# A selective-scan image network: operands of the scan moved by eight bytes, one third of the products on GpSimd, the remainder of B from TensorE

## The chip, the cores and the metric

The kernel runs on one core of a Trainium2 chip. The metric is the device time of one execution in microseconds (us), the median of several runs. TensorE (PE in the profile) multiplies matrices into PSUM, VectorE (DVE), ScalarE (ACT) and GpSimd (POOL) work on tiles in the on-chip memories, and SyncE (SP) issues the transfers here. Each engine takes its own instructions in order and waits on semaphores for those of the others.

## The reference

Four images of 56 x 56 tokens with 96 channels go through four layers. Layers 0 and 1 each run a selective scan over the tokens in four orders (by rows or by columns, forward or reversed); layers 2 and 3 are linear attention and a small network in a reduced float format. The scan is nearly all of the time. For each of the 192 inner channels d and 16 states s it computes, token by token:

```
dt = softplus(dt_raw @ dtw.T + dtb)          # a size per token and channel
a  = -exp(A_log)                             # a number per channel and state
h  = exp(dt * a) * h + dt * B[s] * u         # the recurrence over tokens
y  = sum over s of h * C[s]                  # plus u * D
```

dt_raw, B and C are linear functions of u, by a matrix of their own for each order.

## The kernel before

**Tiling.** The scan of a layer, image and order is cut into 7 chunks of 448 tokens: 2 layers x 4 images x 4 orders x 7 = 224 chunks. A chunk has 8 rounds: two halves e of 96 channels by four quarters q of the states. A round covers 96 x 4 pairs of channel and state, which lie on 128 partitions in three groups g of 448 tokens (32 channels by 4 states a group). There are 1792 rounds and 5376 scans.

**A round.** `begin` has TensorE spread B over the partitions into the PSUM tile b (`spread_b`, L580; there is one such tile) and makes the tile v of three rows with CS + 2 = 450 elements, of which the tokens are 1 to 448 (TOKENS) and the outer two take the carried state. VectorE multiplies dt*u (du) by b into v for groups 0 and 1 (L673). The third group's product is made ahead by GpSimd from B in SBUF (half 1 of the tile cb, L651), except in the rounds named by OWN, where VectorE makes it as well: 3, 4 and 6 of the eight, or 3 and 4 in images 1 to 3 of layer 1. ScalarE makes the decay exp(dt * a) of each group in the PSUM tiles da (`decay`, L643; one tile a group, so that the decay of a round waits for the scan of the round before). VectorE scans the three groups in place in v (L699). ScalarE keeps the last column (L703) and puts it beside the next chunk's tokens (`carried`, L658). GpSimd multiplies all three groups by C into hc (L709), and TensorE sums hc over the states into y two rounds later (`add_up`, L737). In every fourth round ScalarE moves y to Y (`keep_sums`, L744).

**A chunk's preparation** is laid over the rounds of the chunks before it (`prepare`, `prepare_on_scalar`, `prepare_ahead`). TensorE projects u to the rows of B, C and dt_raw (L428, in the one PSUM tile pp); ScalarE copies them to cf (L467, L469). Rows 64 to 127 of cf hold what is needed of B for `spread_b`, which multiplies cf as bfloat16 (its upper halves): a part as it is, and, in the rows where GpSimd has taken the upper half away (`split`, L593, two instructions a chunk), the remainder, so that the sum keeps B's precision. TensorE makes dt's argument from 12 or 6 rows of cf (`step_size`, L480), ScalarE makes dt from it with Exp and Ln (`softplus`, L489 and L490), and GpSimd multiplies it by u (`times_u`, L496), each twice a chunk, once for each half e. dt and dt*u go to DRAM (`park`, L506) and come back spread over 128 partitions (`spread`, L513), C and B likewise (`fetch`, L521, four transfers for each q).

**Order.** Every engine's instructions stand in the order in which the generator `scans` records them; SP's transfers too. At two places of a round it yields to side work: the other layers' work on other images (`load`, `middle`, `fuse`, `attend`), which is cut into pieces with estimated costs on ScalarE and TensorE. `spend` and `room` let a piece in where the costs of the round leave room. `keep_busy` fills TensorE's spare time with matmuls by zeros (L724), in number WARM less the estimated work. Side work left over when the scans end is done alone, in the tail.

Of the kernel before, what the change touches and what calls it, by code (L numbers as in the profile page):

```python
# [11 lines left out]
F32 = mybir.dt.float32  # L12
# [21 lines left out]
TOKENS = slice(1, CS + 1)  # L34
# [4 lines left out]
OWN = (3, 4, 6)  # L39
OWN_TAIL = (3, 4)  # L40
# [7 lines left out]
WARM, PER_P = 7.3, 1.6  # L48
# [116 lines left out]
class Net:  # L165
    def __init__(self, ctx, tc, aps, at, out):
# [14 lines left out]
        self.U = [self.big.tile([C, L], F32, name=f"U{e}") for e in range(NE)]  # L181
# [65 lines left out]
    def setup(self):  # L247
# [95 lines left out]
        with tc.tile_pool(name="stage", bufs=1) as st:  # L343
# [10 lines left out]
            self.some = self.upper(self.tiles["w128"][:, :CS])  # L354
            self.zeros = const.tile([128, C], BF16, name="zeros")
# [103 lines left out]
    def rows(self, ch):  # L459
# [5 lines left out]
        ch.cf = sp.tile([128, CS], F32, name="cf")  # L465
# [5 lines left out]
    def step_sizes(self, ch):  # L471

        nc = self.nc
        ch.cd = self.dram.tile([2 * NS, CS], F32, tag="cd", name="cd", bufs=3)
        nc.sync.dma_start(ch.cd, ch.cf[: 2 * NS])
        ch.pd = [self.step_size(ch, 0, self.pp())]

    def step_size(self, ch, e, ps):
        rows = slice(32, 32 + RANK[ch.l])
        self.nc.tensor.matmul(ps[:C], ch.par.wt[rows, C * e : C * e + C], ch.cf[rows], start=True, stop=True)  # L480
        return ps[:C]

    def softplus(self, ch, e):

        dt = self.sp.tile([C, CS], F32, name="dtc")
        self.nc.scalar.activation(dt, ch.pd[e], AF.Exp, bias=ch.par.dtb[:, e : e + 1])  # L489
        self.nc.scalar.activation(dt, dt, AF.Ln, bias=1.0)  # L490
        ch.dtc.append(dt)

    def times_u(self, ch, e):

        du = self.sp.tile([C, CS], F32, name="duc")
        self.nc.gpsimd.tensor_tensor(  # L496
            du.rearrange("p (a b) -> p a b", b=HS),
            ch.dtc[e].rearrange("p (a b) -> p a b", b=HS),
            self.in_order(self.U[e], ch.orient, ch.c * CS, CS),
            ALU.mult,  # L500
        )
        ch.duc.append(du)

    def park(self, l, t):
        d = self.dram.tile([C, CS], F32, tag="dd", name="dd", bufs=8)
        self.nc.sync.dma_start(d, t)  # L506
        l.append(d)

    def spread(self, l, d, name):

        t = self.sp.tile([128, NG, CS], F32, name=name)
        for s in range(4):
            self.nc.sync.dma_start(t[32 * s : 32 * s + 32], d.rearrange("(g d) t -> d g t", d=32))  # L513
        l.append(t)
# [9 lines left out]
    def prepare(self, ch, follow, r):  # L524

        if r == 0:
            self.spread(ch.du, ch.dud[1], "du")
            self.spread(ch.dt, ch.dtd[1], "dt")
            self.fetch(ch, 3)
        if follow is None:  # L530
            return
        if r == 1:
            self.step_sizes(follow)
            self.split(follow, 0)
        elif r == 2:
            self.split(follow, 1)
        elif r == 3:
            follow.pd.append(self.step_size(follow, 1, self.pp()))
            self.times_u(follow, 0)
            self.park(follow.dtd, follow.dtc[0])  # L540
        elif r == 4:
            self.times_u(follow, 1)
            self.park(follow.dtd, follow.dtc[1])
            self.park(follow.dud, follow.duc[0])
            self.spread(follow.dt, follow.dtd[0], "dt")
        elif r == 5:
            self.park(follow.dud, follow.duc[1])
            self.spread(follow.du, follow.dud[0], "du")
        if r > 4:
            self.fetch(follow, r - 5)  # L550

    def prepare_on_scalar(self, follow, r):

        if follow is None:
            return
# [778 lines left out]
```

## Time and profile before

| what | value |
|---|---|
| median of 3 runs (lowest, highest) | 8497.21 us (8489.68, 8497.39) |
| span of the profiled execution | 8506.0 us |
| first scan starts, last scan ends | 120 us, 8158 us |
| a chunk of 8 rounds, mean | 35.9 us |
| VectorE busy | 7810.2 us |
| GpSimd busy | 7589.0 us |
| TensorE busy, ScalarE busy | 7442.0 us, 5928.4 us |
| time of the main queue's packets, share of the 16 DMA engines' span | 69.2% |

The profiled execution took 8506.0 us, 9 us over the median. The busy time of an engine is the time in which at least one of its instructions ran; on VectorE the end of one instruction and the start of the next overlap a little. A line of a group reads: source line, engine, operation, output <- inputs with partitions x elements, count, then busy time and mean ns of one, then the engine's idle time just before them and what ended it. A line of waits reads: engine and line that waited, for whom, then us in total, how often, the longest. A line of a stretch has its start and end, its length, then busy us and instruction count for TensorE, its weight loads, VectorE, ScalarE and GpSimd, the granted TensorE clock, the share of the DMA engines and GB/s. A line of the timeline has start, length, engine, line and how many instructions were merged.

### The profile page before, as it was taken

The numbers are of one execution on the slowest core, as the hardware profiler recorded it, in microseconds if no ns is written. First come the engines' busy times: TensorE is split into PE (matmuls) and PEld (weight loads), VectorE is DVE, ScalarE is ACT, GpSimd is POOL, SyncE is SP. The second block draws the span as 40 slices with busy tenths as digits, with TensorE's granted clock in tenths as the row PEclk, the third lists the DMA queues.
The fourth block names the chain that finished last, engine by engine and source line by source line (L and its number), as shares of the span: only waits on it lengthen the run. The fifth ranks groups of instructions, "written<-read, shape, count | busy, mean of one in ns | idle before, by whom it ended". The sixth has DMA issues, their size and how long they took to land. (4 is left out here: it accounts for less than half of the span.)

```text
span 8506.0 us, 120303 instructions
## 1 busy us (share of the span) xinstructions
PE 7442.0 (87%) x33459; PEld 2707.3 (32%) x33459; DVE 7810.2 (92%) x10142; ACT 5928.4 (70%) x12597; POOL 7589.0 (89%) x4075
## 2 busy tenths in 40 slices
PE   6888888898889888898889988998899888998997
PEld 3222223232333223232233223333333333333345
DVE  5999999999999999999999999999999999999941
ACT  5877667676777657776677755667766777667746
POOL 4989999999999999999999999999999999999930
PEclk8888889898999889998899988999899898998986
DMA  5777677677777777776777777666776777767731
GB/s 142 167 186 186 164 186 182 153 173 168 189 172 179 163 182 175 178 171 161 184 180 176 166 174 171 165 164 165 185 177 160 165 173 185 178 156 166 175 83 45
DMA packets 951337, 1417.87 MB, mean 167 GB/s; under 512 B 176578, under 2 KB 943812, under 8 KB 949796
## 3 DMA queue, kind: packets, MB, share of 16 engines
q1 hardware_dynamic: 949888, 1408.37, 69.2%
q8 instruction: 263, 4.31, 0.2%
q14 instruction: 414, 3.39, 0.1%
q10 hardware_dynamic: 772, 1.80, 0.1%
HBM read 1141.42 MB, written 268.14 MB: 166 GB/s over the span
## 5 line engine op out<-in xcount | busy, mean ns | idle before, releaser
L699 DVE TENSOR_TENSOR_SCAN v<-da,v 128x449 f32<-128x449 f32 (+1 forms) x5376 | 5507.6, 1072 | 62.2 <-ACT v L658 36.2
L709 POOL TENSOR_TENSOR hc<-v,cb 128x1344 f32<-128x1344 f32 x1792 | 5166.6, 2884 | 366.5 <-DVE v L699 230.8
L643 ACT ACTIVATE da<-dt,na 128x448 f32<-128x448 f32 x5376 | 3392.7, 633 | 1409.7 <-DVE v L699 1372.7
L673 DVE TENSOR_TENSOR v<-du,b 128x448 f32<-128x448 f32 x4172 | 2331.4, 605 | 164.7 <-PE b L580 68.4
L737 PE MATMUL y<-hc,four 128*32 128x448 f32 x14336 | 1942.7, 617 | 3.7 <-POOL hc L709 3.6
L651 POOL TENSOR_TENSOR v<-du,cb 128x448 f32<-128x448 f32 x1204 | 1373.4, 1141 | 102.0 <-DMA cb<-cd 45.6
L724 PE MATMUL y<-w,zeros 128*96 128x448 bf16 x5117 | 1443.3, 399 | 0.0
L580 PE MATMUL b<-cf,sel 128*128 128x448 bf16 x1792 | 685.2, 382 | 861.9 <-DVE v L673 856.3
L724 PEld LDWEIGHTS <-zeros 128*96 128x96 bf16 x5117 | 631.2, 134 | 1300.0 <-issue 1142.7
L428 PE MATMUL pp<-U,wd 96*128 96x448 f32 x896 | 671.2, 836 | 13.7 <-DMA U<-u 13.7
L737 PEld LDWEIGHTS y<-hc,four 128*32 128x32 f32 x14336 | 297.0, 114 | 1206.0 <-issue 816.8
L733 PE MATMUL y<-Y,ident 96*96 96x448 f32 x672 | 540.2, 893 | 52.2 <-ACT Y L744 33.0
L496 POOL TENSOR_TENSOR duc<-dtc,U 96x448 f32<-96x448 f32 x448 | 559.2, 1248 | 5.1 <-ACT dtc L490 5.1
L881 PE MATMUL ps<-win,dg 64*64 64x220 f32 (+9 forms) x1962 | 507.9, 453 | 0.0
L480 PE MATMUL pp<-cf,wd 12*96 12x448 f32 (+1 forms) x896 | 484.3, 622 | 0.4 <-ACT cf L467 0.4
L703 ACT COPY carry<-v 128x3 f32<-128x3 f32 x1536 | 298.7, 194 | 262.4 <-DVE v L699 260.0
L489 ACT ACTIVATE dtc<-pp,wd 96x448 f32<-96x448 f32 x448 | 279.0, 623 | 273.9 <-PE pp L480 272.7
L593 POOL TENSOR_TENSOR cf<-cf 64x448 f32<-64x448 f32 x448 | 417.1, 931 | 35.3 <-ACT cf L467 0.3
L744 ACT COPY Y<-y 96x448 f32<-96x448 f32 x448 | 339.5, 758 | 39.2 <-PE y L737 37.4
L881 PEld LDWEIGHTS ps<-win,dg 64*64 64x64 f32 (+2 forms) x1962 | 229.7, 158 | 326.2 <-issue 267.4
L580 PEld LDWEIGHTS <-sel 128*128 128x128 bf16 x1792 | 186.7, 104 | 348.9 <-issue 284.5
L733 PEld LDWEIGHTS y<-Y,ident 96*96 96x96 f32 x672 | 116.5, 184 | 550.1 <-ACT da L643 244.2
(411 smaller groups left out, 5954.0 us busy)
## 6 DMA issues: line engine op xcount, KB each, us to landing
cb<-cd SPq DMA_DIRECT2D x3584, 112.0 KB, 4.3
dt<-dd SPq DMA_DIRECT2D x1792, 168.0 KB, 4.3
du<-dd SPq DMA_DIRECT2D x1792, 168.0 KB, 4.2
dd<-dtc SPq DMA_DIRECT2D x448, 168.0 KB, 2.0
dd<-duc SPq DMA_DIRECT2D x448, 168.0 KB, 2.1
U<-u SPq DMA_DIRECT2D x112, 168.0 KB, 4.7
z<-w SPq DMA_DIRECT2D x56, 224.0 KB, 3.2
u<-w SPq DMA_DIRECT2D x56, 224.0 KB, 3.5
```

The source lines that it names most:

```text
L428: self.nc.tensor.matmul(ch.ps.rearrange("p (a b) -> p a b", b=HS), ch.par.wx[:, e], self.in_order(self.U[e], ch.orient, ch.c * CS, CS), st ...
L496: self.nc.gpsimd.tensor_tensor(du.rearrange("p (a b) -> p a b", b=HS), ch.dtc[e].rearrange("p (a b) -> p a b", b=HS), self.in_order(self.U ...
L580: self.nc.tensor.matmul(ps, self.sel[:, q], self.upper(ch.cf), start=True, stop=True)
L643: nc.scalar.activation(da[g][:, TOKENS], ch.dt[e][:, g], AF.Exp, scale=ch.par.na[:, e, q, g : g + 1])
L651: nc.gpsimd.tensor_tensor(v[:, 2, TOKENS], ch.du[e][:, 2], ch.cb[q][:, 1], ALU.mult)
L673: nc.vector.tensor_tensor(v[:, g, TOKENS], ch.du[e][:, g], b, ALU.mult)
L699: nc.vector.tensor_tensor_scan(v[:, g, way], da[g][:, way], v[:, g, way], 0.0, ALU.mult, ALU.add)
L709: nc.gpsimd.tensor_tensor(hc, v[:, :, TOKENS], ch.cb[q][:, 0].unsqueeze(1).to_broadcast([128, NG, CS]), ALU.mult)
L724: self.nc.tensor.matmul(self.y[:C], self.zeros, self.some, start=False, stop=False)
L733: nc.tensor.matmul(o, w, self.in_order(a, ch.orient, ch.c * CS, CS), start=True, stop=False)
L737: nc.tensor.matmul(self.y[32 * n : 32 * n + 32], self.four, hc[:, g], start=n == 3, stop=n == 3 or q == NQ - 1,)
L881: self.nc.tensor.matmul(o[:, a - r0 : e - r0, x0:x1], diag[:, tap], win[:, a + dy - lo : e + dy - lo, x0 + dx : x1 + dx], start=n == 0, st ...
```

## The change

- **Places.** The tile of a round is now h: one row of 1352 elements a partition, in which group g's tokens begin at element 450 g + 2, so eight bytes into the tile; neighbouring groups share the columns between them. dt*u (du) and dt (dtc) get two elements in front by `shifted`; the tiles of C and B (cb), u, hc and the spread dt stay as they are. The scans and da move by one element too (INNER).
- **Third group.** OWN and OWN_TAIL are empty: GpSimd makes the third group's product in all 1792 rounds (L686 of the new file), VectorE two a round (L691).
- **Remainder of B.** `split` is gone. TensorE subtracts the upper half of cf from the projection still standing in PSUM (`less`, a bfloat16 matmul by minus the identity, L586), and ScalarE copies rows 64 to 127, and a round later rows 96 to 127, again to cf (L573). cf has three buffers and is made two rounds earlier.
- **dt*u in one.** The two halves of dt lie in one tile; Exp is made for each half, Ln and the product with u once for both (L491, L504), and each is parked in one transfer.
- **Schedule.** `prepare` is told the round's distance o to the chunk's first round, in place of separate steps for this chunk, the next and the one after. WARM is 6.8 in place of 7.3, and the costs that `spend` is told for the rounds differ. The scratch space for transfers in the compiler's call is made smaller.

```diff
 CR = CW // HS
 NCW = L // CW
 CS = 448
-TOKENS = slice(1, CS + 1)
+ROW = CS + 2
+WIDE = NG * ROW + 2
+INNER = slice(2, CS + 2)
 NCS = L // CS
 RANK = (12, 6)
 NW, LATE_NW = 13, 20
 NWIN = 3
-OWN = (3, 4, 6)
-OWN_TAIL = (3, 4)
+OWN = ()
+OWN_TAIL = ()
 SPARE = (0.9, 2.4)
...
-WARM, PER_P = 7.3, 1.6
+WARM, PER_P = 6.8, 1.6
...
+            self.minus = const.tile([128, 64], BF16, name="minus")
+            nc.vector.tensor_scalar(self.minus[64:], self.ident[64:, 64:], -1.0, None, ALU.mult)
...
-        ch.cf = sp.tile([128, CS], F32, name="cf")
+        ch.cf = sp.tile([128, CS], F32, name="cf", bufs=3)
...
-    def step_sizes(self, ch):
-        nc = self.nc
-        ch.cd = self.dram.tile([2 * NS, CS], F32, tag="cd", name="cd", bufs=3)
-        nc.sync.dma_start(ch.cd, ch.cf[: 2 * NS])
-        ch.pd = [self.step_size(ch, 0, self.pp())]
-    def step_size(self, ch, e, ps):
+    def step_size(self, ch, e):
         rows = slice(32, 32 + RANK[ch.l])
-        self.nc.tensor.matmul(ps[:C], ch.par.wt[rows, C * e : C * e + C], ch.cf[rows], start=True, stop=True)
-        return ps[:C]
+        ch.pd = self.pp()[:C]
+        self.nc.tensor.matmul(ch.pd, ch.par.wt[rows, C * e : C * e + C], ch.cf[rows], start=True, stop=True)
     def softplus(self, ch, e):
-        dt = self.sp.tile([C, CS], F32, name="dtc")
-        self.nc.scalar.activation(dt, ch.pd[e], AF.Exp, bias=ch.par.dtb[:, e : e + 1])
-        self.nc.scalar.activation(dt, dt, AF.Ln, bias=1.0)
-        ch.dtc.append(dt)
-    def times_u(self, ch, e):
-        du = self.sp.tile([C, CS], F32, name="duc")
-        self.nc.gpsimd.tensor_tensor(
-            du.rearrange("p (a b) -> p a b", b=HS),
-            ch.dtc[e].rearrange("p (a b) -> p a b", b=HS),
-            self.in_order(self.U[e], ch.orient, ch.c * CS, CS),
-            ALU.mult,
-        )
-        ch.duc.append(du)
-    def park(self, l, t):
-        d = self.dram.tile([C, CS], F32, tag="dd", name="dd", bufs=8)
-        self.nc.sync.dma_start(d, t)
-        l.append(d)
-    def spread(self, l, d, name):
-        t = self.sp.tile([128, NG, CS], F32, name=name)
+        scalar = self.nc.scalar
+        if e == 0:
+            ch.dtc = self.shifted(C, NE, "dtc", 1)
+        scalar.activation(ch.dtc[:, e], ch.pd, AF.Exp, bias=ch.par.dtb[:, e : e + 1])
+        if e == NE - 1:
+            scalar.activation(ch.dtc, ch.dtc, AF.Ln, bias=1.0)
+    def shifted(self, rows, n, name, bufs=2):
+        t = self.sp.tile([rows, 2 + n * CS], F32, name=name, bufs=bufs)
+        return t[:, 2:].rearrange("p (n t) -> p n t", t=CS)
+    def times_u(self, ch):
+        ch.duc = self.sp.tile([C, NE, CS], F32, name="duc", bufs=1)
+        u = self.both.rearrange("p e (h w) -> p e w h" if ch.orient else "p e (h w) -> p e h w", w=HS)
+        lo = ch.c * CS // HS
+        in_rows = lambda t: t.rearrange("p e (a b) -> p e a b", b=HS)
+        self.nc.gpsimd.tensor_tensor(in_rows(ch.duc), in_rows(ch.dtc), u[:, :, lo : lo + CS // HS], ALU.mult)
+    def park(self, t):
+        d = self.dram.tile([NE, C, CS], F32, tag="dd", name="dd", bufs=6)
+        self.nc.sync.dma_start(d.rearrange("e p t -> p e t"), t)
+        return d
+    def spread(self, t, d):
         for s in range(4):
             self.nc.sync.dma_start(t[32 * s : 32 * s + 32], d.rearrange("(g d) t -> d g t", d=32))
-        l.append(t)
+    def spread_dt(self, ch, e):
+        ch.dt.append(self.sp.tile([128, NG, CS], F32, name="dt"))
+        self.spread(ch.dt[e], ch.dtd[e])
+    def spread_du(self, ch, e):
+        ch.du.append(self.shifted(128, NG, "du"))
+        self.spread(ch.du[e], ch.dud[e])
+    def groups(self, t, at):
+        return t[:, at : at + NG * ROW].rearrange("p (g t) -> p g t", t=ROW)
...
+    def prepare(self, ch, o):
+        nc = self.nc
+        if o == -14:
+            self.parameters(ch)
+        elif o == -12:
+            self.inputs(ch)
+        elif o == -9:
+            ch.cd = self.dram.tile([2 * NS, CS], F32, tag="cd", name="cd", bufs=3)
+            nc.sync.dma_start(ch.cd, ch.cf[: 2 * NS])
+            self.less(ch, 64)
+        elif o == -8:
+            self.less(ch, 96)
+        elif o in (-7, -6):
+            self.step_size(ch, o + 7)
+        elif o == -5:
+            self.times_u(ch)
+            ch.dtd = self.park(ch.dtc)
+        elif o == -4:
+            ch.dud = self.park(ch.duc)
+            self.spread_dt(ch, 0)
+        elif o == -3:
+            self.spread_du(ch, 0)
+        elif o == 0:
+            self.spread_du(ch, 1)
+            self.spread_dt(ch, 1)
+        if -3 <= o <= 0:
+            self.fetch(ch, o + 3)
+    def prepare_on_scalar(self, ch, o):
+        if o == -10:
+            self.rows(ch)
+        elif o in (-9, -8):
+            part = slice(64 if o == -9 else 96, 128)
+            self.nc.scalar.copy(ch.cf[part], ch.ps[part])
+        elif o in (-7, -6):
+            self.softplus(ch, o + 7)
+    def projected(self, ch, o):
+        return () if o not in (-12, -11) else (o + 12,) if not ch.first else (0, 1) if o == -11 else ()
+    def less(self, ch, at):
+        self.nc.tensor.matmul(
+            ch.ps[at:], self.minus[at:, at - 64 :], self.upper(ch.cf[at:]), start=False, stop=True, skip_group_check=True
+        )
...
-    def split(self, ch, n):
-        x = ch.cf[64 + 32 * n :]
-        self.nc.gpsimd.tensor_tensor(x, x, self.upper(x), ALU.subtract)
...
-        da = [self.psum.tile([128, 512], F32, name=f"da{g}")[:, : CS + 2] for g in range(NG)]
+        da = [self.psum.tile([128, 512], F32, name=f"da{g}")[:, : CS + 4] for g in range(NG)]
...
+                nc.scalar.activation(da[g][:, INNER], ch.dt[e][:, g], AF.Exp, scale=ch.par.na[:, e, q, g : g + 1])
...
+        def column(t, at):
+            return t[:, at : at + 2 * ROW + 1 : ROW]
+        def carried(n):
+            if n < len(rounds) and rounds[n][0].step:
+                ch, e, q = rounds[n]
+                nc.scalar.copy(column(hs[n], ROW if ch.rev else 1), ch.par.carry[:, e, q])
+        def kept(n):
             ch, e, q = rounds[n]
+            if ch.step < NCS - 1:
+                nc.scalar.copy(ch.par.carry[:, e, q], column(hs[n], 2 if ch.rev else CS + 1))
+        def own(n):
+            ch, e, q = rounds[n]
+            return NQ * e + q in (OWN_TAIL if ch.l and ch.i else OWN)
+        hs, bs = {}, {}
+        def tokens(t):
+            return self.groups(t, 2)[:, :, :CS]
         def begin(n):
+            if n < len(rounds):
+                ch, e, q = rounds[n]
+                bs[n] = self.spread_b(ch, q)
+                hs[n] = sp.tile([128, WIDE], F32, name="h", bufs=3)
+                if not own(n):
+                    nc.gpsimd.tensor_tensor(tokens(hs[n])[:, 2], ch.du[e][:, 2], ch.cb[q][:, 1], ALU.mult)
+        def products(n):
             ch, e, q = rounds[n]
+            for g in range(3 if own(n) else 2):
+                nc.vector.tensor_tensor(tokens(hs[n])[:, g], ch.du[e][:, g], bs[n], ALU.mult)
+        def scan(n, g):
             ch, e, q = rounds[n]
+            c = 1 if ch.step else 0
+            way = slice(CS + 1 + c, 1, -1) if ch.rev else slice(2 - c, CS + 2)
+            h = hs[n][:, g * ROW :]
+            nc.vector.tensor_tensor_scan(h[:, way], da[g][:, way], h[:, way], 0.0, ALU.mult, ALU.add)
...
             self.half_round()
-            far = afters.get(ch)
             strided = [1.5 + 1.5 * ch.orient] * (r % NQ == 2)
-            if far and self.projected(far, r) in (0, 1):
-                strided.append(1.5 + 1.5 * far.orient)
-            self.spend((0.7, 0, 1.3, 1.3, 0, 0, 0, 0)[r], 1.3 * (r in (1, 3)) + sum(strided))
+            ahead(n, lambda c, _: strided.append(1.5 + 1.5 * c.orient))
+            self.spend((0.6, 0.7, 1.7, 0, 0, 0, 0.7, 0.6)[r], (0.4, 1.3, 1.3, 0, 0, 0, 0, 0.4)[r] + sum(strided))
             yield "F", n, r
-            self.prepare_on_scalar(nexts.get(ch), r)
...
             hc = sp.tile([128, NG, CS], F32, name="hc", bufs=3)
-            nc.gpsimd.tensor_tensor(hc, v[:, :, TOKENS], ch.cb[q][:, 0].unsqueeze(1).to_broadcast([128, NG, CS]), ALU.mult)
+            nc.gpsimd.tensor_tensor(
+                hc, tokens(hs[n]), ch.cb[q][:, 0].unsqueeze(1).to_broadcast([128, NG, CS]), ALU.mult,
+            )
...
-    nc = _bacc.Bacc("TRN2", target_bir_lowering=False, num_devices=1)
+    nc = _bacc.Bacc("TRN2", target_bir_lowering=False, num_devices=1, dynamic_dma_scratch_size=4096)
```

## The prediction

> **What bounds the kernel now.** I read the engines' busy times first, then the table by stretches, the costliest groups, the waits of VectorE, and a timeline of 5 us for what an instruction costs back to back.
>
> ```profile
> PE 7442.0 (87%) x33459; PEld 2707.3 (32%) x33459; DVE 7810.2 (92%) x10142; ACT 5928.4 (70%) x12597; POOL 7589.0 (89%) x4075
> ```
>
> Two engines are nearly full. The stretches show where they are not:
>
> ```profile
> 0.00:120.00 120.00, 81.07 (x247) 46.54 (x248) 19.45 (x86) 49.35 (x76) 12.55 (x20) 0.82 0.44 123
> ...
> 4000.00:5000.00 1000.00, 871.97 (x3863) 291.64 (x3862) 968.09 (x1239) 708.71 (x1449) 937.81 (x494) 0.91 0.74 175
> ...
> 8158.00:8506.00 348.00, 298.86 (x1293) 184.72 (x1291) 48.78 (x91) 179.75 (x409) 27.93 (x25) 0.75 0.17 45
> ```
>
> The third pair of columns is VectorE: 0.97 of each us between the first scan (120) and the last (8158). The head of 120 us and the tail of 348 us are other work. The body is 8038 us; VectorE is busy there for 7810 - 19 - 49 = 7742, so idle for 296; GpSimd for 7549, idle for 489. The waits of VectorE are small and scattered, and hardly any is on GpSimd:
>
> ```profile
> DVE v L673 <- PE b L580: 68.4, 88, 4.3
> DVE v L699 <- ACT v L658: 36.2, 64, 4.1
> ...
> DVE v L699 <- POOL v L651: 21.2, 28, 1.9
> ```
>
> So VectorE sets the pace, with GpSimd 2.4% behind it. The groups of both:
>
> ```profile
> L699 DVE TENSOR_TENSOR_SCAN v<-da,v 128x449 f32<-128x449 f32 (+1 forms) x5376 | 5507.6, 1072 | 62.2 <-ACT v L658 36.2
> L709 POOL TENSOR_TENSOR hc<-v,cb 128x1344 f32<-128x1344 f32 x1792 | 5166.6, 2884 | 366.5 <-DVE v L699 230.8
> L673 DVE TENSOR_TENSOR v<-du,b 128x448 f32<-128x448 f32 x4172 | 2331.4, 605 | 164.7 <-PE b L580 68.4
> L651 POOL TENSOR_TENSOR v<-du,cb 128x448 f32<-128x448 f32 x1204 | 1373.4, 1141 | 102.0 <-DMA cb<-cd 45.6
> L496 POOL TENSOR_TENSOR duc<-dtc,U 96x448 f32<-96x448 f32 x448 | 559.2, 1248 | 5.1 <-ACT dtc L490 5.1
> L593 POOL TENSOR_TENSOR cf<-cf 64x448 f32<-64x448 f32 x448 | 417.1, 931 | 35.3 <-ACT cf L467 0.3
> ```
>
> Durations of neighbours overlap, so I take VectorE's real price from runs in a row:
>
> ```profile
> 4002.24 3.05 DVE L699 TENSOR_TENSOR_SCAN v<-da,v 128x449 f32<-128x449 f32 x3
> ...
> 4005.21 1.66 DVE L673 TENSOR_TENSOR v<-du,b 128x448 f32<-128x448 f32 x3
> ```
>
> One more product costs (1.66 - 0.605) / 2 = 0.53 us, one more scan 0.99.
>
> **What the skill says.** GPSIMD Engine Reference, section 3.1: the two read streams share one port, about 2.5 cycles an element are called the floor, and 2048 elements took 4497 ns. Here (2884 - 1141) / 896 = 1.95 ns an element, somewhat below that, and the two rows lie differently. SBUF — State Buffer, Specifications: lines of 16 bytes, two hits on a line are needed for full rate, each crossing pays. No page says that two streams in step pay more than two out of step; the trace of before has a hint: L593, the same operation on as many elements with both inputs in the same bytes, takes 931 ns against 1141. Same page, Who interferes with whom: a VectorE instruction with one input in SBUF doesn't contend with GpSimd. VectorE's products and scans have their other input in PSUM, and every one of L709 takes between 2852 and 2927 ns whatever VectorE does, so I count no contention.
>
> **The change, part by part** (profiled execution, body unless said).
>
> VectorE loses the third product of the rounds in OWN: 4172 - 2 x 1792 = 588 instructions x 0.53 = 312 us, leaving 7742 - 312 = 7430. Nothing else of it changes; scans and products start eight bytes on instead of four, which I cost at nothing (its aligned products L818 have 600 ns against 605).
>
> GpSimd loses both halves of the split, 417 us. It gains 588 x 1.141 = 671. One product of 896 elements in place of two of 448 saves a fixed part, 1141 - 448 x 1.95 = 270 ns, 224 times: 60 us. At the old rates: 7549 - 417 + 671 - 60 = 7743.
>
> The offset is the unknown. Before, h lies 4 bytes off C, and dt*u and B lie in step; after, all pairs are 8 bytes apart or 16 and 24 (the rows of h advance by 1800 bytes). Lower bound: the 210 ns that L593 has less for 448 elements, at every product: 4 x 210 = 0.84 us a round, 1505 us in all. Upper bound: nothing gained; a loss I leave out, since h at 4 bytes off costs no more per element than the aligned rows. I take half, 753 us: h about 1.04 us, hc about 2.57. Then GpSimd has 6990, well under VectorE's 7430. Balance is reached with 313 of the 1505, about a fifth.
>
> ScalarE gains two copies from PSUM a chunk, 448 x 0.52 (L469, 521 ns) = 233 us, and loses between 0 and 129 by one Ln of 896 in place of two at 577 ns. It stays under 80%: hidden behind scans, since it waits 1373 us for VectorE before decays.
>
> TensorE gains 448 short matmuls at 0.38 (as L580) = 171 us; filler matmuls go from 5117 to 5061 in the built programs, -22. 7591 of 8200 is 93% by modelled ends; it now waits 856 us for VectorE's products before b, which is the cover. If that goes, b comes late and VectorE's 68 us grow.
>
> DMA: half as many parks with the same bytes; dt and du are sent out in the same rounds. SP's order has one late point: B and C of the fourth quarter are fetched in the chunk's first round, behind eight transfers of du and dt, and the fourth round's third product was VectorE's. Now GpSimd needs it a round and a half earlier. By start times it has 8 us in the median chunk, 4.3 in the worst twentieth, against 4.3 to land. I put 0.5 us of GpSimd waiting a chunk, 112 us, hidden while GpSimd has 450 to spare. A stalled product also holds the hc behind it, and after that y on TensorE.
>
> Head: two more hops in the first chunk's chain, +5 us. Tail: the built program has some 12% more rows after the last scan (side work is given less room per round); 348 x 0.12 = 42 at most, I take 25.
>
> Sum: 7430 + 296 idle as before + 120 + 5 + 348 + 25 = 8224 for a profiled execution. The one of before has 8506 against a median of 8497, so 8215.
>
> **Rivals.**
> (a) *GpSimd gains the whole bound.* 6240 busy; VectorE's waits behind it (v 21, idle slots after stalls) shrink, at best idle falls to 150: 8070. For it: 931 is measured. Against: that row reads one line for both streams, not two lines out of step.
> (b) *The offset does nothing and GpSimd becomes the bound: slower.* 7743 busy. With VectorE's present idle 296 the body is 8039, as now; with GpSimd's own present idle 489 it is 8232. Middle 8135, and +30 + 468 = 8633; it decides when less than about a fifth of the 1505 is gained. For it: rows of 448 and 1344 fit one line of constant rate although one is in step and the other is not; the skill calls the rate a floor.
> (c) *A small gain*, a tenth to a quarter of the bound, GpSimd and VectorE level at 7430 to 7600 and each waiting for the other: 8330 to 8480.
> (d) *The longer chain for B's remainder.* Four hops TensorE to ScalarE a chunk in place of two. Today ScalarE waits 272.7 us for 448 such hops, 0.61 each; 448 more are 273 us, and if decays were late by all of it: 8215 + 273 = 8490. Against: scans wait for da only 3.9 us in the whole run.
>
> **How the numbers follow.** VectorE stays the bound (half the gain and (a) together): 0.70, with 8215 likeliest and 8050 to 8320 its own range. (c) 0.10, (d) 0.05, (b) 0.15. The range 8050 to 8490 leaves out most of (b), and a few hundredths below. Faster by over 0.2% (about what a measurement can tell here; 17 us): 0.70 + 0.10 + half of (d) - a little = 0.80; within: 0.04, from (c), (d) and the low end of (b); slower: 0.16, nearly all (b).
>
> **What would show it.** Right: GpSimd's hc row near 2.57 us and its product near 1.04; 3584 products on VectorE at about 605; VectorE at 96% in the body, GpSimd near 90% or less; head and tail within 50 us of now. Wrong: hc at 2.85 to 2.9 with GpSimd over 95% and VectorE's scans waiting for h from GpSimd (b); ScalarE's waits on pp above 500 us and scans waiting for da (d); GpSimd waiting for cb over 300 us. A DMA slowed by the eight-byte start of du would show in its time to land, 4.2 us now.

## The result, and the profile after

The changed kernel takes 8575.0 us (median of 4 runs, 8559.5 to 8577.0) against 8497.3 us; the ratio is 1.0087 with a 95% interval of 1.0072 to 1.0102. It is slower by 0.9%, outside the range that was forecast (8050 to 8490) and on the other side.

The engines' busy times and the body of the changed kernel's profile, in the same columns as before (the second line is the stretch from the first scan to the last, the third is the tail):

```profile
PE 7605.2 (89%) x33851; PEld 2757.7 (32%) x33851; DVE 7521.8 (88%) x9555; ACT 6085.3 (71%) x12807; POOL 7185.1 (84%) x3991
```

```profile
112.60:8187.20 8074.60, 7200.90 (x32177) 2512.35 (x32176) 7447.13 (x9364) 5835.03 (x12274) 7145.02 (x3947) 0.90 0.70 171
8187.20:8573.60 386.40, 330.26 (x1424) 203.29 (x1424) 54.44 (x104) 198.78 (x454) 29.89 (x27) 0.74 0.18 47
```

Both engines that were nearly full have lost what they were meant to lose: VectorE is busy for 7447 us in the body (7742 before), GpSimd for 7145 (7549). But the body has grown from 8038 to 8075 us. VectorE idles there for 8074.6 - 7447.1 = 627 us, in place of 296. The span is 67.6 us longer: 37 in the body, 39 in the tail (386 against 348), 8 less in the head.

The groups say in front of what it idles:

```profile
L739 POOL TENSOR_TENSOR hc<-h,cb 128x1344 f32<-128x1344 f32 x1792 | 4883.2, 2725 | 826.4 <-DVE h L698 601.0
L698 DVE TENSOR_TENSOR_SCAN h<-da,h 128x449 f32<-128x449 f32 (+1 forms) x5376 | 5502.3, 1071 | 44.8 <-POOL h L686 37.8
...
L691 DVE TENSOR_TENSOR h<-du,b 128x448 f32<-128x448 f32 x3584 | 2039.9, 606 | 516.4 <-ACT h L662 407.9
...
L686 POOL TENSOR_TENSOR h<-du,cb 128x448 f32<-128x448 f32 x1792 | 1752.9, 978 | 103.7 <-DMA cb<-cd 96.6
...
L662 ACT COPY h<-carry 128x3 f32<-128x3 f32 x1536 | 290.2, 189 | 630.1 <-POOL h L686 620.9
```

GpSimd's products are faster than before (2725 against 2884 ns, 978 against 1141), as half-expected. VectorE's products (L691) now stand still for 516 us, 408 of them for ScalarE's copy of three carried columns (L662). That copy waits in its turn for GpSimd's product of the third group (L686). No such wait is in the profile before: there, the products waited 68 us for b, and the copy (L658 there) for 2 us in all:

```profile
L658 ACT COPY v<-carry 128x3 f32<-128x3 f32 x1536 | 277.3, 181 | 2.0 <-POOL hc L709 0.8
```

The two rows of the changed kernel's list of waits:

```profile
ACT h L662 <- POOL h L686: 620.9, 529, 7.0
...
DVE h L691 <- ACT h L662: 407.9, 337, 6.2
```

A timeline of one round in a reversed chunk shows the chain in order:

```profile
3568.63 1.77 POOL L504 TENSOR_TENSOR duc<-dtc,U 96x896 f32<-96x896 f32 x1
...
3569.74 0.59 DVE L691 TENSOR_TENSOR h<-du,b 128x448 f32<-128x448 f32 x1
...
3570.36 0.97 POOL L686 TENSOR_TENSOR h<-du,cb 128x448 f32<-128x448 f32 x1
...
3571.36 0.20 ACT L662 COPY h<-carry 128x3 f32<-128x3 f32 x1 [0.46 <-POOL h L686]
...
3571.59 0.62 DVE L691 TENSOR_TENSOR h<-du,b 128x448 f32<-128x448 f32 x1 [1.26 <-ACT h L662]
```

VectorE ends its product for group 0 at 3570.33 and could go on with group 1, for which du and b are there. It goes on at 3571.59, after GpSimd has ended the product for group 2 (3571.33) and ScalarE the copy. The dt*u for both halves, now one instruction and here of 1.77 us, stood ahead of GpSimd's product and pushed it back by as much.

None of the three touches what another touches. In the old tile v, of shape 128 x 3 x 450, the carried column was `v[:, :, at : at + 1]` and a group's tokens `v[:, g, TOKENS]`; the program kept them apart. In the new tile h, one row of 1352 elements, the carried columns are `h[:, at : at + 901 : 450]`, a slice with a step. My theory was that this slice is taken as the whole stretch from its first to its last column: 1 to 901 for a forward chunk, which covers the tokens of groups 0 and 1, and 450 to 1350 for a reversed one, which covers those of groups 1 and 2. The waits in the built program (the list of each engine's instructions, with what each one waits for) stand exactly so: in the 768 rounds of forward chunks that have a carried state the first product waits for the copy, in the 768 of reversed chunks the second, and in these the copy waits for GpSimd's third product as well. None of them is in the program before. I call this the false wait.

The timeline above shows one kind of it only. Set beside the order of the rounds in the program, the 337 waits of VectorE for the copy fall into three:

| waits of VectorE for the copy | how often | us |
|---|---|---|
| reversed chunk, the copy itself waited for GpSimd | 88 | 117 |
| reversed chunk, the copy waited for no other engine just before it | 91 | 104 |
| forward chunk (there the copy doesn't need GpSimd's product of its round) | 158 | 187 |

In the second and third kind the copy is late because ScalarE is: it stands in ScalarE's order behind side work or the preparation of later chunks. A forward chunk shows it; between the scans of two rounds ScalarE loads activation tables (L801 is the second load) and does two pieces of side work, then the decay, then the copy:

```profile
1251.62 1.28 ACT L801 ACT_TABLE_LOAD   x1
...
1252.91 0.64 ACT L652 ACTIVATE da<-dt,na 128x448 f32<-128x448 f32 x1
...
1253.58 0.20 ACT L662 COPY h<-carry 128x3 f32<-128x3 f32 x1
...
1253.81 1.15 DVE L691 TENSOR_TENSOR h<-du,b 128x448 f32<-128x448 f32 x2 [1.56 <-ACT h L662]
```

In the kernel before, only the scans need the copy, and they come after the products.

### The profile page after: what moved, and what is told of

It reads as the page before. It is cut to its first block, busy times and chain, and to the rows that moved or that the text cites. A ratio compares the mean times of both kernels' runs of the same rounds, so it can differ in the third digit from the quotient of the medians.

```text
span 8573.6 us, 119867 instructions
## 1 busy us (share of the span) xinstructions
PE 7605.2 (89%) x33851; PEld 2757.7 (32%) x33851; DVE 7521.8 (88%) x9555; ACT 6085.3 (71%) x12807; POOL 7185.1 (84%) x3991
## 5 line engine op out<-in xcount | busy, mean ns | idle before, releaser
L739 POOL TENSOR_TENSOR hc<-h,cb 128x1344 f32<-128x1344 f32 x1792 | 4883.2, 2725 | 826.4 <-DVE h L698 601.0
L698 DVE TENSOR_TENSOR_SCAN h<-da,h 128x449 f32<-128x449 f32 (+1 forms) x5376 | 5502.3, 1071 | 44.8 <-POOL h L686 37.8
L691 DVE TENSOR_TENSOR h<-du,b 128x448 f32<-128x448 f32 x3584 | 2039.9, 606 | 516.4 <-ACT h L662 407.9
L686 POOL TENSOR_TENSOR h<-du,cb 128x448 f32<-128x448 f32 x1792 | 1752.9, 978 | 103.7 <-DMA cb<-cd 96.6
L757 PE MATMUL y<-w,zeros 128*96 128x448 bf16 x5061 | 1410.0, 399 | 0.0
L593 PE MATMUL b<-cf,sel 128*128 128x448 bf16 x1792 | 680.4, 380 | 788.3 <-DVE h L691 782.0
L662 ACT COPY h<-carry 128x3 f32<-128x3 f32 x1536 | 290.2, 189 | 630.1 <-POOL h L686 620.9
L504 POOL TENSOR_TENSOR duc<-dtc,U 96x896 f32<-96x896 f32 x224 | 482.3, 2153 | 4.5 <-ACT dtc L491 4.5
L667 ACT COPY carry<-h 128x3 f32<-128x3 f32 x1536 | 295.0, 192 | 175.6 <-DVE h L698 172.4
L573 ACT COPY cf<-pp 64x448 f32<-64x448 f32 x448 | 235.6, 526 | 180.8 <-PE pp L586 172.1
L593 PEld LDWEIGHTS <-sel 128*128 128x128 bf16 x1792 | 181.8, 101 | 417.4 <-issue 352.5
```

The source lines that it names most:

```text
L504: self.nc.gpsimd.tensor_tensor(in_rows(ch.duc), in_rows(ch.dtc), u[:, :, lo : lo + CS // HS], ALU.mult)
L593: self.nc.tensor.matmul(ps, self.sel[:, q], self.upper(ch.cf), start=True, stop=True)
L686: nc.gpsimd.tensor_tensor(tokens(hs[n])[:, 2], ch.du[e][:, 2], ch.cb[q][:, 1], ALU.mult)
L691: nc.vector.tensor_tensor(tokens(hs[n])[:, g], ch.du[e][:, g], bs[n], ALU.mult)
L698: nc.vector.tensor_tensor_scan(h[:, way], da[g][:, way], h[:, way], 0.0, ALU.mult, ALU.add)
L739: nc.gpsimd.tensor_tensor(hc, tokens(hs[n]), ch.cb[q][:, 0].unsqueeze(1).to_broadcast([128, NG, CS]), ALU.mult,)
```

## The experiments

Ratios are to the kernel before, run again beside each experiment (medians 8492 to 8500 us). Lines left out of an edit are marked by three dots.

**1. The false wait taken away, and with it the step between rows (rows452).** h becomes a tile of three rows of 452 elements, each with its own outer columns:

```diff
-ROW = CS + 2
-WIDE = NG * ROW + 2
+ROW = CS + 4
...
-            return t[:, at : at + 2 * ROW + 1 : ROW]
+            return t[:, :, at : at + 1]
...
-                nc.scalar.copy(column(hs[n], ROW if ch.rev else 1), ch.par.carry[:, e, q])
+                nc.scalar.copy(column(hs[n], CS + 2 if ch.rev else 1), ch.par.carry[:, e, q].unsqueeze(2))
...
-            return self.groups(t, 2)[:, :, :CS]
+            return t[:, :, INNER]
...
-                hs[n] = sp.tile([128, WIDE], F32, name="h", bufs=3)
+                hs[n] = sp.tile([128, NG, ROW], F32, name="h", bufs=3)
...
-            h = hs[n][:, g * ROW :]
+            h = hs[n][:, g]
```

> The changed kernel with h as a tile of three rows of 452 elements in place of one row of 1352, so that each group has columns of its own for the carried state; all else as changed. In the built program VectorE's products then wait for TensorE's b alone and ScalarE's copy of the carried column no longer for GpSimd's product of the same round. Theory 'false wait' (the columns of the one-row tile are taken as one stretch that covers the tokens): VectorE's 408 us of waiting for that copy and ScalarE's 621 us for GpSimd go, VectorE's idle in the body falls from 633 to about 300, the time to 8200 to 8260. Rival 'GpSimd or its order is the limit anyway': the waits are put down to another and the time stays within 40 us of 8575. On the rate: with 'half a line' the product by C falls from 2.72 to about 2.56 us, else it stays.

Measured: 8312.9 us, 0.979 of the kernel before (0.9775 to 0.9804), 262 us below the changed kernel and 53 over the top of what was expected. The body is 7819 us with VectorE busy for 7434, so it idles for 385 and not for about 300. The waits for the copy before the products are gone. But this edit also made the product by C faster (2565 ns), so experiment 5 separates the two.

**2. The order of the writers alone (carry_early).** The tile stays as changed; the copy is issued before GpSimd's product:

```diff
                 hs[n] = sp.tile([128, WIDE], F32, name="h", bufs=3)
+                carried(n)
                 if not own(n):
...
                 decay(n + 1, g)
-                if g == 0:
-                    carried(n + 1)
```

> The changed kernel with the copy of the carried columns issued before GpSimd's product of the same round, in place of after the first decay. The tile and what is taken as its stretch stay; only the order in which the three writers of h stand changes: ScalarE's copy no longer waits for GpSimd's product, GpSimd's product and VectorE's products wait for the copy. Theory 'false wait': the loop from GpSimd through ScalarE to VectorE opens, VectorE's waits for the copy fall from 408 to under 100 us, time 8230 to 8350. Rival 'ScalarE is late for other reasons, the link to GpSimd is not what counts': the waits stay above 300, time 8500 to 8600.

Measured: 8349.3 us, 0.9831 (0.9816 to 0.9845), at the top of what was expected. VectorE's products still wait 149 us for the copy (under 100 was expected), GpSimd's products 121:

```profile
DVE h L692 <- ACT h L662: 149.4, 184, 5.2
...
POOL h L687 <- ACT h L662: 121.1, 113, 5.2
```

The overlap is still taken for real, but the copy no longer stands between GpSimd and VectorE. The edit does a second thing: it also sets the copy ahead of the round's decays in ScalarE's order. So it doesn't tell how much each of the two brought.

**3. The kernel before with all third products on GpSimd (before_all).**

```diff
-OWN = (3, 4, 6)
-OWN_TAIL = (3, 4)
+OWN = ()
+OWN_TAIL = ()
```

> The kernel before with OWN and OWN_TAIL empty, and nothing else: GpSimd makes all third products at the old places. GpSimd's busy time in the body rises by 588 x 1.141 = 671 us to 8220. Theory 'GpSimd would have been the bound without the offset and the remainder': 8750 to 8900 us. Rival 'VectorE stays the bound': VectorE loses 312 us, 8190 to 8250.

Measured: 8766.0 us, 1.0324 (1.0307 to 1.0342). GpSimd is busy for 8166 of the body's 8314 us. Its list of waits shows what a GpSimd bound looks like, and it isn't what the changed kernel shows: the scans wait for GpSimd's product directly.

```profile
DVE v L699 <- POOL v L651: 543.5, 624, 6.2
DVE v L673 <- PE b L580: 87.0, 101, 4.8
```

**4. What an offset costs, by itself (offsets).** GpSimd works alone, 16 instructions of each kind, in one run:

```diff
...
+    for n, t in enumerate(moved):
+        for _ in range(16):
+            nc.gpsimd.tensor_tensor(o[:, 0], t[:, n : n + CS], c, ALU.mult)
+    for t in rows:
+        for _ in range(16):
+            nc.gpsimd.tensor_tensor(o, t, by_three, ALU.mult)
+    for n in (0, 2):
+        for _ in range(16):
+            t = moved[n][:, n : n + 3 * CS].rearrange("p (g t) -> p g t", t=CS)
+            nc.gpsimd.tensor_tensor(o, t, by_three, ALU.mult)
...
```

> The disputed cost by itself: GpSimd alone multiplies 448 elements of a tile at 0, 4, ... 32 bytes off by an aligned row, 16 times each, then three rows of 448 by one repeated row with the rows at steps of 1792, 1800 and 1808 bytes; nothing of the scan is computed. Theory 'half a line': 8 and 24 bytes off cost about 0.98 us and 0, 16 and 32 about 1.14, with 4 and 12 between; three rows at steps of 1808 bytes (all 8 or 24 off) cost about 2.56 us, at 1800 (8, 16, 24) 2.72, in step 3.05. Rival 'any distance but 0 in 32': 16 costs 0.98 like 8, and steps of 1808 bytes cost 2.72 like 1800. Rival 'one rate, a fixed part': rows in step cost 2.88 as the product of before.

The n-th moved tile is read from 4n bytes on; the other input, c, starts at a multiple of 16 bytes throughout. In the groups of this kernel the name of the moved tile is this distance in bytes, or the kind of its rows (steps 1800, half 1808 bytes apart, both from byte 8; four: 1800 from byte 4; the first line has three rows 1792 bytes apart from byte 0):

```profile
L50 POOL TENSOR_TENSOR o<-movedzero,cb 128x1344 f32<-128x1344 f32 x16 | 48.2, 3011 | 1.3
L46 POOL TENSOR_TENSOR o<-rowsfour,cb 128x1344 f32<-128x1344 f32 x16 | 45.8, 2862 | 1.2
L46 POOL TENSOR_TENSOR o<-rowssteps,cb 128x1344 f32<-128x1344 f32 x16 | 43.3, 2708 | 1.3
L46 POOL TENSOR_TENSOR o<-rowshalf,cb 128x1344 f32<-128x1344 f32 x16 | 41.0, 2565 | 1.3
...
L43 POOL TENSOR_TENSOR o<-movedzero,cb 128x448 f32<-128x448 f32 x16 | 18.1, 1129 | 5.4 <-DVE movedzero L30 4.3
...
L43 POOL TENSOR_TENSOR o<-movedsixteen,cb 128x448 f32<-128x448 f32 x16 | 18.0, 1126 | 1.2
L43 POOL TENSOR_TENSOR o<-movedfour,cb 128x448 f32<-128x448 f32 x16 | 18.0, 1122 | 1.2
...
L43 POOL TENSOR_TENSOR o<-movedtwelve,cb 128x448 f32<-128x448 f32 x16 | 15.6, 975 | 1.3
...
L43 POOL TENSOR_TENSOR o<-movedeight,cb 128x448 f32<-128x448 f32 x16 | 15.6, 975 | 1.3
```

Two levels, and a period of 16 bytes: 8, 12, 24 and 28 bytes take 975 ns, 0, 4, 16, 20 and 32 take 1122 to 1129. I call the second kind in step, the first out of step. "Half a line" was right on 8, 16, 24 and 32. It was wrong on 4, which gains nothing, and on 12, which gains all; both were expected in between. Three rows 1792 bytes apart from byte 8, all out of step, take 2562 ns. Each row of 448 that is out of step is worth 150 ns, so the product by C is explained row by row: before, its rows lay 4, 12 and 20 bytes off, one of three out of step (2862 here, 2884 in the kernel); in the changed kernel 8, 16 and 24, two of three (2708; 2725); with rows at steps of 1808 bytes, all (2565; 2565).

**5. The false wait and the rate, apart (rows450x4, flat452).** rows450x4 keeps every element where the change has put it, but in a tile of four rows of 450, where the carried column of a reversed chunk is the first of the next row. flat452 keeps the one-row tile and takes the faster step.

```diff
# rows450x4
...
-            return t[:, at : at + 2 * ROW + 1 : ROW]
+            g, at = divmod(at, ROW)
+            return t[:, g : g + NG, at : at + 1]
...
-                hs[n] = sp.tile([128, WIDE], F32, name="h", bufs=3)
+                hs[n] = sp.tile([128, NG + 1, ROW], F32, name="h", bufs=3)
...
# flat452
-ROW = CS + 2
+ROW = CS + 4
...
-                nc.scalar.copy(column(hs[n], ROW if ch.rev else 1), ch.par.carry[:, e, q])
+                nc.scalar.copy(column(hs[n], CS + 2 if ch.rev else 1), ch.par.carry[:, e, q])
...
```

> The changed kernel with h as a tile of four rows of 450 elements (the fourth only for its first column), so that every element lies where it lay and GpSimd's rate stays at 2.72 us; only what the program takes as overlapping is exact. Theory 'false wait' alone: VectorE's 408 us of waiting for the copy go, 8310 to 8370 us. Rival 'the gain of rows of 452 came from GpSimd's faster product by C': 8480 to 8580.

> The changed kernel with h as one row with groups at steps of 452 elements: GpSimd's product by C takes 2.57 us as in the kernel with rows of its own, and the columns of the carried state are still taken as one stretch that covers tokens. Theory 'false wait': the loop from scan over GpSimd and ScalarE to VectorE gets 0.16 us a round shorter and no more, VectorE still waits 150 to 350 us for the copy, 8380 to 8520 us. Rival 'the rate is what counts': 8300 to 8340.

| us, median (ratio to before, interval) | one row, false wait | rows of their own |
|---|---|---|
| steps of 450, product by C 2.73 us | 8575.0 (1.0087; 1.0072 to 1.0102) | 8321.6 (0.9792; 0.9772 to 0.9812) |
| steps of 452, product by C 2.57 us | 8528.6 (1.0045; 1.0027 to 1.0064) | 8312.9 (0.979; 0.9775 to 0.9804) |

rows450x4 came out as expected; flat452 is 9 us over the top of its range. The false wait costs 253 us at one rate and 216 at the other. The faster product by C brings 46 us where the false wait stands; without it the 9 us are within the noise. In flat452 VectorE waits for the copy nearly as long as in the changed kernel, and more than the 150 to 350 us expected:

```profile
DVE h L691 <- ACT h L662: 381.3, 330, 5.1
```

Body of rows450x4, and its groups:

```profile
112.10:7927.90 7815.80, 7078.45 (x32177) 2478.24 (x32176) 7433.86 (x9364) 5862.27 (x12274) 7133.11 (x3947) 0.92 0.72 177
```

```profile
L698 DVE TENSOR_TENSOR_SCAN h<-da,h 128x449 f32<-128x449 f32 (+1 forms) x5376 | 5504.8, 1071 | 148.8 <-ACT h L662 77.7 <-POOL h L686 60.3 <-ACT da L651 9.0
...
L691 DVE TENSOR_TENSOR h<-du,b 128x448 f32<-128x448 f32 x3584 | 2016.7, 603 | 146.5 <-PE b L592 103.2 <-DMA du<-dd 36.6 <-DMA cb<-cd 2.3
...
L662 ACT COPY h<-carry 128x3 f32<-128x3 f32 x1536 | 283.9, 185 | 11.4 <-POOL hc L739 1.0
```

The copy waits 11 us in place of 630, the products 147 in place of 516. VectorE's and GpSimd's busy times are those of the changed kernel; only the idle time went, from 627 to 7816 - 7434 = 382 us. Of the 408 us at the copy only 245 come back: the scans, which need the copy in truth, now wait 78 us for it, and 60 for GpSimd's third product (38 in the changed kernel); the products wait 103 for b (67).

**6. The offset undone (in_step).** From rows452, with h, dt*u and dt sixteen bytes off:

```diff
-ROW = CS + 4
-INNER = slice(2, CS + 2)
+ROW = CS + 8
+INNER = slice(4, CS + 4)
...
-        t = self.sp.tile([rows, 2 + n * CS], F32, name=name, bufs=bufs)
-        return t[:, 2:].rearrange("p (n t) -> p n t", t=CS)
+        t = self.sp.tile([rows, 4 + n * CS], F32, name=name, bufs=bufs)
+        return t[:, 4:].rearrange("p (n t) -> p n t", t=CS)
...
```

> The kernel with rows of its own for each group, but with h, dt*u and dt sixteen bytes off in place of eight (rows of 456 elements), so that GpSimd's two inputs are in step in every product; all else the same. Theory 'half a line': the product by C takes 3.01 us in place of 2.57, the third group's 1.13 in place of 0.98, GpSimd's busy time in the body rises by 1792 x 0.60 = 1070 us and something for dt*u to about 7980, GpSimd becomes the bound, 8540 to 8680 us. Rival 'the eight bytes gave only what GpSimd had idle anyway': below 8400.

Measured: 8664.0 us, 1.019 (1.0175 to 1.0206), as expected for in step:

```profile
L734 POOL TENSOR_TENSOR hc<-h,cb 128x1344 f32<-128x1344 f32 x1792 | 5493.2, 3065 | 87.6 <-DVE h L693 62.4 <-DMA du<-dd 10.4 <-PE ps L790 5.9
L681 POOL TENSOR_TENSOR h<-du,cb 128x448 f32<-128x448 f32 x1792 | 2083.8, 1163 | 86.0 <-DMA cb<-cd 81.9 <-DMA y<-Y 2.5 <-DMA z<-w 1.5
```

GpSimd is busy for 7999 of 8164 us. So without the offset all third products on GpSimd cost time even with B's remainder gone; with it they save time. The offset is worth 351 us to rows452 (8664.0 - 8312.9).

**7. B's remainder left out (no_remainder).** From rows452, without `less` and without the two copies a chunk.

```diff
-            self.less(ch, 64)
-        elif o == -8:
-            self.less(ch, 96)
...
-        elif o in (-9, -8):
-            part = slice(64 if o == -9 else 96, 128)
-            self.nc.scalar.copy(ch.cf[part], ch.ps[part])
```

> The kernel with rows of its own for each group, without the two matmuls and the two copies a chunk that make B's remainder: b is then summed from the upper halves of the whole rows, a part of the computation is changed. Rival of the prediction 'the longer chain for the remainder delays ScalarE and through it VectorE': ScalarE's 181 us of waiting for pp at the copies go, VectorE's waits for the carried column (79 us) and for b (116) fall back to those of before (36 and 68), 8210 to 8270 us. Theory 'it is hidden': within 25 us of 8313.

Measured: 8282.0 us, 0.9742 (0.9723 to 0.9761), 31 us below rows452, between the two expectations. VectorE's wait for b fell from 116 to 87 us, that for the carried column from 79 to 67. The chain is nearly hidden where the false wait is gone; its 31 us are not what made the change slow.

**8. The costs told to the planner of side work (old_costs).** From rows452, with the `spend` line of before:

```diff
-            self.spend((0.6, 0.7, 1.7, 0, 0, 0, 0.7, 0.6)[r], (0.4, 1.3, 1.3, 0, 0, 0, 0, 0.4)[r] + sum(strided))
+            self.spend((0.7, 0, 1.3, 1.3, 0, 0, 0, 0)[r], 1.3 * (r in (1, 3)) + sum(strided))
```

> The kernel with rows of its own for each group, with the costs that the side work's planner is told for the rounds as before (0.7, 0, 1.3, 1.3 on ScalarE, 1.3 on TensorE in rounds 1 and 3). Theory 'the longer tail is side work that the new costs put off': the tail falls from 385 to about 348 us, in all 8265 to 8290. Rival 'more room for side work costs VectorE in the body what the tail gains': 8300 to 8330.

Measured: 8300.4 us, 0.9763 (0.9748 to 0.9778). The tail falls from 385 to 335 us and the body grows by 28. So the time is what the rival had (8300 to 8330), and the tail what the theory had. The longer tail of the changed kernel is side work put off, and about half of it is paid in the body when the tail is spared it; the two medians are 12 us apart, and the intervals of their ratios overlap.

**9. One more product on GpSimd (also6), and the copy early as well (early_old, early_old_also6).** also6 is rows452 with

```diff
+ALSO = (6,)
...
-                if not own(n):
-                    nc.gpsimd.tensor_tensor(tokens(hs[n])[:, 2], ch.du[e][:, 2], ch.cb[q][:, 1], ALU.mult)
+                g = 1 if NQ * e + q in ALSO else 2
+                nc.gpsimd.tensor_tensor(
+                    tokens(hs[n])[:, g:], ch.du[e][:, g:],
+                    ch.cb[q][:, 1].unsqueeze(1).to_broadcast([128, NG - g, CS]), ALU.mult,
+                )
...
-            for g in range(3 if own(n) else 2):
+            for g in range(1 if NQ * e + q in ALSO else 2):
```

early_old is rows452 with the edits of experiments 2 and 8, early_old_also6 all of these.

> The kernel with rows of its own for each group, where GpSimd also makes the second group's product in the seventh round of each chunk, in one instruction of 896 elements. VectorE loses 224 x 0.53 = 119 us, GpSimd gains 224 x 0.74 = 166 (it is 87% busy in the body). Theory 'VectorE is the bound again': 8190 to 8260 us. Rival 'the order of GpSimd's work counts, not its sum': the longer instruction holds back the product by C behind it, and nothing is gained, 8300 to 8340.

> Rows of its own for each group, the costs of the rounds as before, and the copy of the carried column issued before GpSimd's product of the same round. VectorE's scans waited 125 us for that copy with these costs; if ScalarE has it done a half round earlier, 8190 to 8250 us; if another wait takes its place, 8280 to 8310.

> The same, with the second group's product of the seventh round on GpSimd too. VectorE has 119 us less to do; alone this gave 16. If waits and not VectorE's work set the pace by now, 0 to 30 us below the kernel without it; if VectorE is the bound, 80 to 119 below.

Measured: also6 8297.0 us, 0.9761 (0.9742 to 0.978); early_old 8308.6 us, 0.9783 (0.9766 to 0.9799); early_old_also6 8275.9 us, 0.974 (0.9724 to 0.9756). The first two came out as their rivals had it (also6 just below its 8300 to 8340), the third 33 us below early_old. In also6 VectorE is busy 97 us less (7337 against 7434) and idles 79 more (464 against 385): work taken from it now turns mostly into waits. The early copy gave nothing: the scans' wait of 125 us for it (old_costs) is replaced by one of 135 for the decays behind it on ScalarE. early_old_also6 is 221 us below the kernel before and 299 below the changed one, the fastest that ran.

## Why the prediction was wrong

**The step that failed** stands in the part on VectorE: "Nothing else of it changes", and in the sum "296 idle as before". It took the move of h into one row for a matter of places in memory, and asked what it does to GpSimd's rate and to the length of VectorE's instructions, not what the program has to take as overlapping. The edit added a wait on ScalarE's copy to 1536 rounds of 1792, behind which VectorE's queue stands, and a wait on GpSimd to the copy in reversed chunks. Measured: 408 us of VectorE's idle time at that wait, 253 us of the total (rows450x4). No rival had it. It could have been seen beforehand: the built program lists what each instruction waits for, and VectorE's products wait there for ScalarE's copy, which they do not in the program before.

**What made the wait dear** is in the main that ScalarE has the copy done late, and in part GpSimd. The false wait asks for the copy before a round's products in place of before its scans, two products or some 1.06 us earlier (in reversed chunks one product, 0.53 us). What stands ahead of the copy on ScalarE then lands on VectorE: 291 of the 408 us are of this kind (104 + 187). The other 117 come through GpSimd, in a loop of reversed chunks: scan, product by C, third product, copy, VectorE's second product, scans, over two rounds. By the durations, with 0.14 us between a scan and GpSimd's start and 0.03 at each change of engine about the copy, it takes 0.14 + 2.73 + 0.98 + 0.03 + 0.19 + 0.03 + 0.53 + 3 x 0.99 = 7.60 us, against 2 x (2 x 0.53 + 3 x 0.99) = 8.06 us that VectorE needs for two rounds by itself. Half a microsecond of slack is enough for the loop, but not for a dt*u ahead of the third product (2.15 us in the mean): it stood there in 71 of the 88 waits, with 99 of the 117 us. That flat452, with 0.16 us less in the loop, is only 46 us faster agrees with this. This sorting is read from what stood just before each wait. A delay can also be the late effect of an earlier one (in reversed chunks ScalarE itself idles 621 us before the copy), so the shares are not costs that runs have shown one by one.

**The steps, one by one.**
- VectorE's busy time: 7430 forecast, 7447 measured. Right.
- GpSimd's products: 1.04 and 2.57 forecast, 978 ns and 2725 measured. The third product gained 163 ns of the 210 of the bound, the product by C 159 of 630: of its three rows one was out of step already, and one, 16 bytes off, which I took as moved, is in step (experiment 4). The 210 ns themselves were misread: L593 reads its second input as bfloat16, which the reading left out, and a row out of step gains 150. The sum came out near: 6990 forecast, 7145 measured, and it left GpSimd idle for 929 us in the body. It gained (0.163 + 0.159) x 1792 = 577 of the 1505, more than the fifth at which the two engines balance.
- "h at 4 bytes off costs no more per element than the aligned rows" was right by luck: one row of three was already out of step. The single rate of 1.95 ns an element that I drew from two rows mixed two rates. From experiment 4 they are (3011 - 1129) / 896 = 2.10 ns in step and (2562 - 975) / 896 = 1.77 out of step. The figure that I took from the Trainium skill (GPSIMD Engine Reference, section 3.1: 4497 ns for 2048 elements) fits the rate in step: 1129 + 1600 x 2.10 = 4489. By the 1.2 GHz that the page reckons with, an estimate, 2.10 ns are 2.5 cycles and 1.77 ns 2.1. So what the page calls a floor (about 2.5 cycles in its section 2.1, about 2.6 in 3.1) is near the rate in step; out of step it was passed here.
- ScalarE: copies 233 forecast, 236 measured; the one Ln takes 952 ns, so 448 x 0.577 - 224 x 0.952 = 45 us are saved, within the bounds. Waits for pp at the four hops of a chunk: 172 + 102 = 274 us against 273 before at two; rival (d) fell (31 us in experiment 7).
- Late C and B: 112 us forecast, GpSimd's product waits 97 for them against 46 before. Right in kind, half in size.
- Head +5 forecast, -8 measured; tail +25 forecast, +39 measured. Experiment 8 shows the tail's cause as I had it.
- Rival (b), GpSimd as the bound, would have given 8633, near the measured time for another reason. Its sign, GpSimd over 95% with the scans waiting for it, is absent: 7145 of 8075 us, 38 us. in_step and before_all show that GpSimd does become the bound where it has all third products and the offset is missing.

With the false wait gone the likeliest case is nearly what ran: the median of rows450x4, 8321.6 us, stands 107 over the 8215 and at the upper edge of that case's range (8050 to 8320). Its profiled span is 8313 us against a sum of 8224. The 89 left are 86 of VectorE's idle time (382 for 296) and 12 of tail, less 13 of head, and what is left over is the 4 us by which VectorE's work was mis-sized. Where the 86 come from is only partly settled. Against the kernel before VectorE waits 35 us more for b (103 for 68), 42 more for the copy before the scans (78 for 36) and 39 more for GpSimd's third product (60 for 21); together that is more than the 86, so smaller waits fell. In rows452 31 us go with the remainder of B (experiment 7). Why each of these waits grew is open.

## What to carry to other kernels

When an edit changes the shape of a tile or writes a slice with a step into it, compare what each instruction waits for in the built program before and after; a wait that nothing in the data asks for holds up what stands behind it in that engine's order, and the busy times will not show it. What it costs depends on how late the engine that is waited for already runs. A saving on the engine that sets the pace is worth its size only if no other engine's result is asked for earlier than before. Where GpSimd is near the limit, try one of its two float32 inputs eight bytes into its tile, and measure.

## What the runs showed of the hardware

GpSimd's products of two float32 inputs have two rates here. With the inputs 8 or 12 bytes apart modulo 16, 448 elements take 975 ns; with 0 or 4 they take 1122 to 1129, whatever the multiple of 16. In the kernel it is the same (978; 1141), with VectorE, ScalarE and TensorE at work. I expected a gain to grow with the distance; it comes whole between 4 and 8 bytes. In every run one of the two inputs starts at a multiple of 16 bytes. Whether the distance counts, or the start of the other input by itself, is therefore not shown; two inputs that both start 8 bytes off would tell.
